# Eleven more tiles turned through DRAM in a linear-attention and NVFP4-GEGLU kernel

## The chip, the core and the metric

The kernel runs on one core of one Trainium2 chip. The metric is device time in microseconds of one execution. Before the change it is 1303.85 us, the median of 3 runs (1300.8 to 1305.99).

## What is computed

Input x has 4 sequences of 512 tokens of width 512. Two pre-norm residual steps are made in float32:

```python
x = x + gated_linear_attention(layernorm(x))     # 4 heads of 128, chunks of 128 tokens
x = x + geglu_mlp(layernorm(x))                  # 512 -> 4096 -> 512, 4-bit weights with scales per block of 32
```

In the attention q, k and v are products of the normed x with 512 x 512 weights; k is scaled to length 1 per head; two gates per head, alpha and beta, come from two further small products. Within a chunk `attn = (q k^T) * beta * decay` and `y_local = attn v`; from chunk to chunk a 128 x 128 state per head is carried, `state = state * total_decay + v^T kw`, and `y = y_local + (q state) * chunk_decay`. In the MLP the weights are unpacked from 4-bit codes, `inter = gelu(x Wg) * (x Wu)`, `out = inter Wd`; every product there is made of three parts (hi, lo, mi) to keep float32 accuracy.

## The kernel before, in words

**Tiles and stages.** All work stands in an order written out by hand; nothing is rescheduled. A counter p numbers the *places*. Each of the 4 sequences b has 12 places: four `product_v`, four `product_q`, four `product_k`. Behind each product, `behind(p)` puts the small work of an earlier chunk: chunk (b, n) has its lead at place 9 + 3 (4b + n), where `chunk_lead` and `chunk_decay` stand, its scores one place later (`chunk_scores`), its sums two places later (`chunk_sums`, which is followed by `second_norm` of the finished rows and by `first_norm` of a tile of the next sequence). From place 45 on the MLP's matmuls take the place of the products, and from about 280 us on the MLP stands alone: 35 rounds of gate, up and down matmuls, with the weights unpacked on VectorE (DVE) and ScalarE (ACT) beside them.

**Turning a tile.** Matmuls contract over the partitions, so a normed tile of 128 tokens x 512 channels must be turned, and k too. Before, there are two ways:

- *On TensorE.* Four `nc.tensor.transpose` into one PSUM bank (L380 for norms, L593 for k), then a copy out of PSUM. All 16 second-norm tiles (`tp_f`) go this way, the 4 first-norm tiles of sequence 0 (`tp_a`), and k of the chunks for which `far(b, n)` is false.
- *Through DRAM.* `cross` writes the tile to DRAM in blocks (one DMA, L310); at the *landing* place it reads it back in four pieces of 64 KB that put 32-row blocks in their turned places (L315); at the *turning* place DVE turns the 32 x 32 blocks (`turn_blocks`, L326). The first-norm tiles of sequences 1 to 3 go this way (`way_a`), and k of chunks 2 and 3 of sequences 0 to 2 (`way_k`).

`cross` books the read at the start of `behind(landing)` (`first_of`) and the turn at its end (`last_of`):

```python
def land():
    t = one_k.get(f"way_{key}")
    for a in range(KC):
        nc.sync.dma_start(f32(t)[:, a * P : (a + 1) * P], way[:, a * 32 : (a + 1) * 32, :])
    last_of.setdefault(turning, []).append(lambda: use(t))
```

A norm that goes through DRAM lands two places after its own and turns three places later. k of a far chunk is written at its product, lands four places ahead of its lead and is turned one place ahead of it.

**Second norm.** `second_norm` (L397 ff.) takes the turned tile, makes its three parts (hi on ACT, L406; lo and mi on DVE, L407 and L408) and stores each to DRAM (`h<-g`, L410). The MLP reads them from there (`x<-h`, L283), the first ones at 202.75 us.

**Queues.** All DMAs are issued by SyncE (SP), in order, on one queue. When a DMA has to wait (the read-back for its write, a store for its data), all later DMAs wait. They run on the core's 16 DMA engines. On SP between 20 and 200 us also stand: x of the next sequences, the residual rows (`xr`) and their write-back (`acc<-xr`), the row sums for the decay (`sums`, read by the exponentials at L608 of the next chunk), the packed MLP weights and their scales, and the h stores. DVE, ACT and TensorE (PE) are in order as well.

**When first norms stand.** `early` (L739 ff.) gives the place of each first norm; for sequence 1 its chunks 0 to 3 stand at places 2, 5, 8 and 8.

Of the kernel before, what the change touches and what calls it, by code (L numbers as in the profile page):

```python
# [35 lines left out]
def f32(t):  # L36
    return t.bitcast(F32)
# [3 lines left out]
def tile_gated_linear_attention__then__nvfp4_geglu(  # L41
# [20 lines left out]
    B, T, D = x.shape  # L62
    H = D // P
    NCH = T // P
# [56 lines left out]
    one_k = Homes("b", 42, [P, T], two_k)  # L121

    def psum(name):
        return fps.tile([P, T], F32, tag="p", name=name)

    def heads(t):
        return t.rearrange("p (h d) -> p h d", d=P)
# [176 lines left out]
    def crossed(t):  # L304
        return t.rearrange("p (w k i) -> p k w i", w=KC, i=32)

    def cross(src, key, use, landing, turning):

        way = dram.tile([KC, P, P], F32, tag=f"way_{key}", name=f"way_{key}")
        nc.sync.dma_start(way.rearrange("w p m -> p w m"), f32(src).rearrange("p (w m) -> p w m", m=P))  # L310
# [7 lines that stand above are left out]
        first_of.setdefault(landing, []).append(land)  # L318

    def turn_blocks(t, *to):  # L320

        new = f32(t).rearrange("p (a k i) -> p k a i", a=KC, i=32)
        done = 0
        for part in to:
            n = part.shape[1]
            nc.vector.transpose(part.rearrange("p k (a j) -> p k a j", j=32), new[:, done : done + n])  # L326
            done += n
        one_k.put(t)

    def norm(src, key, use, parts=1, within=None, way=None):  # L330


        st = small.tile([P, 6], F32, tag="st", name=f"st_{key}")
        nc.vector.bn_stats(st, f32(src))
        if within:
            within()
        mv = small.tile([P, 2], F32, tag="mv", name=f"mv_{key}")
        nc.vector.bn_aggr(mv, st)
        rs = small.tile([P, 1], F32, tag="rs", name=f"rs_{key}")
        nc.vector.tensor_scalar(rs, mv[:, 1:2], 1e-5, None, ALU.add)  # L340
        nc.gpsimd.tensor_tensor(rs, rs, minus_half[:, :1], ALU.pow)

        def settle():

            hn = one_k.get(f"hn_{key}")
            w = D // parts
            if way:
                for c in range(2):
                    nc.vector.tensor_scalar(
                        crossed(f32(hn)).rearrange("p (c two) w i -> p c two w i", c=2)[:, c],  # L350
                        f32(src).rearrange("p (c w i two) -> p c two w i", c=2, w=KC, two=2)[:, c],
                        mv[:, 0:1], rs, ALU.subtract, ALU.mult,
                    )
                one_k.put(src)
                cross(hn, key, way, place[0] + 1, place[0] + 4)
                one_k.put(hn)
                return
            for cols in (slice(i * w, (i + 1) * w) for i in range(parts)):
                nc.vector.tensor_scalar(
                    f32(hn)[:, cols].rearrange("p (c two j) -> p c two j", two=2, j=P),  # L360
                    f32(src)[:, cols].rearrange("p (c j two) -> p c two j", two=2, j=P),
                    mv[:, 0:1], rs, ALU.subtract, ALU.mult,
                )
            one_k.put(src)
            turned.append((hn, key, use))

        settled.append(settle)
# [34 lines left out]
    def second_norm(b, n, src):  # L402
        def use(tp):
            g = [one_k.get(f"g{j}_{b}_{n}") for j in range(3)]
            hi, lo, mi = g
            nc.scalar.activation(hi, tp, AF.Copy, scale=HI)  # L406
            nc.vector.tensor_tensor(lo, tp, f32(hi), ALU.subtract)  # L407
            nc.vector.scalar_tensor_tensor(mi, f32(hi), ONE_E, tp, ALU.mult, ALU.subtract)  # L408
            for j in range(3):
                nc.sync.dma_start(  # L410
                    h2d[b][j][:, :, n * P : (n + 1) * P].rearrange("k p t -> p k t"), heads(f32(g[j]))
                )
            one_k.put(*g)

        norm(src, f"f{b}_{n}", use)


    zs, ss = {}, {}
# [38 lines left out]

    def far(b, n):

        return 1 < n and b < B - 1  # L460

    kTs = {}

    def in_blocks(a):
        return a.rearrange("p (h w i) -> p h w i", h=H, i=32)

    def heads_of(t, blocks):
        return crossed(f32(t)) if blocks else in_blocks(f32(t))

    def product_k(b, n):  # L470

        pk = psum(f"pk_{b}_{n}")
        for k in range(KC):
            nc.tensor.matmul(  # L474
                pk, f32(hT[b][k // 2])[:, k % 2, n * P : (n + 1) * P], f32(wk[k // 2])[:, k % 2, :],
                start=(k == 0), stop=(k == KC - 1),
            )
        kt = one_k.get(f"k_{b}_{n}")
        k_sb[b, n] = kt
        nc.vector.tensor_tensor(heads_of(kt, far(b, n)), in_blocks(pk), in_blocks(f32(bk_sb)), ALU.add)  # L480
        if far(b, n):

            def use(t):
                kT = kTs[b, n] = one_k.get(f"kT_{b}_{n}")
                turn_blocks(t, heads(f32(kT)))

            lead = 2 * NCH + 1 + 3 * (NCH * b + n)
            cross(kt, f"k{b}_{n}", use, lead - 4, lead - 1)
        return lambda: k_factors(b, n, kt)

    def k_factors(b, n, kt):
        sq = one_k.get(f"sq_{b}_{n}")
        sn = small.tile([P, H], F32, tag="ss", name=f"ss{b}_{n}")
        for h in range(H):
            hs = slice(h * P, (h + 1) * P)
            nc.scalar.activation(
                f32(sq)[:, hs].rearrange("p (w i) -> p w i", i=32), heads_of(kt, far(b, n))[:, h],
                AF.Square, accum_out=sn[:, h : h + 1],
            )
        one_k.put(sq)  # L500
        nc.gpsimd.tensor_scalar(sn, sn, 1e-24, None, ALU.max)
        nc.gpsimd.tensor_tensor(sn, sn, minus_half, ALU.pow)
        brn = small.tile([P, H], F32, tag="brn", name=f"brn{b}_{n}")
        nc.gpsimd.tensor_tensor(brn, sn, beta[b][:, n * H : (n + 1) * H], ALU.mult)
        kwf = small.tile([P, H], F32, tag="kwf", name=f"kwf{b}_{n}")
        nc.gpsimd.tensor_tensor(kwf, sn, bdte[b][:, n * H : (n + 1) * H], ALU.mult)
        ss[b, n] = brn, kwf
# [76 lines left out]
    state, ch = {}, {}  # L584

    def chunk_lead(b, n):
        if far(b, n):
            ch["kT"] = kTs.pop((b, n))
            return
        kT = one_k.get(f"kT_{b}_{n}")  # L590
        tp = psum(f"tpk_{b}_{n}")
        for h in range(H):
            nc.tensor.transpose(  # L593
                tp[:, h * P : (h + 1) * P], f32(k_sb[b, n])[:, h * P : (h + 1) * P], ident
            )
        nc.scalar.copy(f32(kT), tp)
        ch["kT"] = kT
# [60 lines left out]
    def chunk_scores(b, n):  # L658
        toks = slice(n * P, (n + 1) * P)
        sp = psum(f"sp_{b}_{n}")  # L660
        kT = ch.pop("kT")
        for h in range(H):
            nc.tensor.matmul(  # L663
                sp[:, h * P : (h + 1) * P], f32(kT)[:, h * P : (h + 1) * P],
                f32(q_sb[b][h // 2])[:, h % 2, toks], start=True, stop=True,
            )
        one_k.put(kT)
        one_k.put(k_sb.pop((b, n)))
        if n == NCH - 1:
            two_k.put(*q_sb[b])  # L670
        if b == B - 1:
            add = state_sums(b, n)
        dm = ch["dm"]
        nc.vector.tensor_tensor(f32(dm), sp, f32(dm), ALU.mult)
        if b == B - 1:
            add()
# [62 lines left out]
    early = {}  # L739
    for b in range(1, B):  # L740
        for n in range(NCH):
            p = 3 * NCH * (b - 1) + 3 * n - 1 if b > 1 else 2 + 3 * min(n, 2)
            early.setdefault(p, []).append((b, n))
    xs = {}

# [6 lines left out]
    def between_steps(p):  # L752

        if p in met:
            return
        met.add(p)
        chunk = chunk_of(p)
        if p % 3 == 0:
            settle()
            if chunk:  # L760
                chunk_lead(*chunk)
                chunk_decay(*chunk)
        elif p % 3 == 1:
            if chunk:
                chunk_scores(*chunk)
            turn("f")
# [8 lines left out]
    def behind(p):  # L775
# [8 lines left out]
        if p % 3 == 0:  # L784
            if left:
                chunk_lead(*chunk)
# [212 lines left out]
    with tc.manual_schedule():  # L999
# [45 lines left out]
        p = 0  # L1045
# [95 lines left out]
```

## Time and profile before

| what | value |
|---|---|
| median of 3 runs | 1303.85 us |
| the profiled execution | 1303.89 us |
| its span, first to last instruction | 1302.2 us |
| mean granted TensorE clock | 0.999 |
| PE busy | 1289.4 us, 99% |
| DVE, ACT, GpSimd (POOL) busy | 968.9, 452.0, 113.6 us |
| `tp_f` matmuls (L380) | 64, four for each of 16 tiles |
| `tpk` matmuls (L593) | 40, four for each of 10 chunks |
| `way_a`, `way_k` writes (L310) | 12 and 6, 256 KB each |
| `way_a`, `way_k` read-backs (L315) | 48 and 24, 64 KB each |
| DVE turns of k (L326, 128 x 512) | 6, median 701 ns |

Matmuls are pipelined, so a row's duration of a matmul is longer than the time from its start to the next one's start; what a matmul takes from the path is read from starts. A view of stretches gives, for each stretch, its length, the busy time of PE, weight loads, DVE, ACT and POOL with the count of instructions, the granted clock, the mean busy share of the 16 DMA engines, and GB/s. A view of waits gives who waited for whom, the sum in us, how often, and the longest.

### The profile page before, as it was taken

Reading aid. Unit: us, or ns where it says so; the run is one execution under the profiler, and the core shown is the slowest. Engines: PE = TensorE matmul, PEld = TensorE weight load, DVE = VectorE, ACT = ScalarE, POOL = GpSimd, SP = SyncE. Lnnn points to the kernel's source line nnn. Section 1 sums busy time; section 2 is a strip of 40 time slices with the busy share of each in tenths; the row PEclk is TensorE's granted clock in tenths of the full one; section 3 lists DMA queues with packets and bytes.
Section 4 is the critical chain, followed back from the end, with each engine's and each line's share of the span. In section 5 each row is a group of like instructions: output and inputs, shape, how many; then the busy total and the mean of one; then the engine's idle time right before and its main releaser. Section 6 shows DMA issues by size and latency. Waiting matters only on the chain.

```text
span 1302.2 us, 17046 instructions
## 1 busy us (share of the span) xinstructions
PE 1289.4 (99%) x5736; PEld 1032.0 (79%) x5736; DVE 968.9 (74%) x1581; ACT 452.0 (35%) x878; POOL 113.6 (9%) x179
## 2 busy tenths in 40 slices
PE   9999999999999999999999999999999999999998
PEld 6567676778888888888888888888888888887886
DVE  3577865888777777777777777777777777777566
ACT  2333335743333333333333333333333333332332
POOL 1536362400000000000000000000000000000000
PEclk9999999999999999999999999999999999999999
DMA  5457677987565656555656565555555555555473
GB/s 195 147 178 195 191 197 214 301 268 235 178 194 178 194 178 194 178 194 179 194 179 193 179 193 179 192 180 192 180 191 181 189 183 189 183 178 198 167 252 127
DMA packets 195383, 250.24 MB, mean 192 GB/s; under 512 B 16672, under 2 KB 93792, under 8 KB 195296
## 3 DMA queue, kind: packets, MB, share of 16 engines
q1 hardware_dynamic: 195296, 249.16, 59.2%
q8 instruction: 45, 0.74, 0.2%
q14 instruction: 42, 0.34, 0.1%
HBM read 191.91 MB, written 57.18 MB: 191 GB/s over the span
## 4 chain that ended last, share of the span: by engine, by line
PE 93%; DMA 3%; DVE 2%; SPq 1%; ACT 1%; issue 0%; POOL 0%; DVEq 0%; ACTq 0%; POOLq 0%
PE pa L853 35%; PE p_d L897 26%; PE pb L853 18%; PE pq L450 4%; PE pk L474 2%; PE pva L425 2%; PE pvb L432 2%; PE yp L717 1%; PE sp L663 1%; PE yp L719 1%; DMA x<-in_x 1%; PE dp L688 1%; DMA pk_d<-in_down_p 1%; PE tp_f L380 0%; DMA x<-h 0%
## 5 line engine op out<-in xcount | busy, mean ns | idle before, releaser
L853 PE MATMUL pa<-x,wgu 128*128 128x512 f32 x2048 | 507.2, 390 | 0.0
L853 PEld LDWEIGHTS pa<-x,wgu 128*128 128x128 f32 x2048 | 384.1, 188 | 79.0
L897 PE MATMUL p_d<-wd,i 128*128 128x512 f32 x1542 | 357.2, 389 | 2.3 <-DVE xr L726 0.6
L897 PEld LDWEIGHTS p_d<-wd,i 128*128 128x128 f32 x1542 | 288.3, 188 | 65.6 <-DVE i L877 2.1
L853 PE MATMUL pb<-x,wgu 128*128 128x512 f32 x1024 | 274.7, 390 | 1.8 <-DMA x<-h 1.8
L858 ACT ACTIVATE t<-pb 128x512 f32<-128x512 f32 x256 | 151.3, 591 | 358.0 <-PE pb L853 353.4
L859 DVE TENSOR_TENSOR t<-pa,t 128x512 f32<-128x512 f32 x256 | 176.6, 690 | 81.2 <-ACT t L858 75.9
L853 PEld LDWEIGHTS pb<-x,wgu 128*128 128x128 f32 x1024 | 192.4, 188 | 42.4 <-DMA x<-h 2.5
L905 DVE SCALAR_TENSOR_TENSOR acc<-p_d,acc 128x512 f32<-128x512 f32 (+1 forms) x137 | 93.4, 682 | 124.8 <-PE p_d L897 123.7
L873 ACT ACTIVATE i<-t 128x512 fp32r<-128x512 f32 x128 | 81.0, 633 | 194.2 <-DVE t L870 189.7
L865 ACT ACTIVATE t<-t 128x512 f32<-128x512 f32 x128 | 81.2, 634 | 136.6 <-DVE t L859 136.5
L877 DVE TENSOR_TENSOR i<-t,i 128x512 fp32r<-128x512 f32 x128 | 88.4, 691 | 25.9 <-ACT i L873 24.1
L909 DVE TENSOR_TENSOR acc<-acc,p_d 128x512 f32<-128x512 f32 x135 | 93.0, 689 | 14.8 <-PE pb L853 0.5
L870 DVE SCALAR_TENSOR_TENSOR t<-t,t 128x512 f32<-128x512 f32 x128 | 88.6, 692 | 4.3
L928 POOL TENSOR_TENSOR acc<-acc,last 128x512 f32<-128x512 f32 x1 | 1.3, 1295 | 1015.0 <-ACT last L927 1015.0
L878 DVE SCALAR_TENSOR_TENSOR i<-i,t 128x512 fp32r<-128x512 f32 x128 | 89.0, 695 | 0.0
L450 PE MATMUL pq<-hT,wq 128*128 128x512 f32 x128 | 57.6, 595 | 0.0
L474 PE MATMUL pk<-wk,hT 128*128 128x512 f32 x128 | 57.4, 593 | 0.0
L450 PEld LDWEIGHTS pq<-hT,wq 128*128 128x128 f32 x128 | 23.6, 191 | 24.1 <-issue 23.9
L474 PEld LDWEIGHTS pk<-wk,hT 128*128 128x128 f32 x128 | 23.3, 191 | 23.9 <-issue 23.9
L183 DVE TENSOR_TENSOR wgu<-wgu,wgu 128x1024 fp32r<-128x1024 f32 x32 | 38.9, 1216 | 0.0
L180 DVE SCALAR_TENSOR_TENSOR wgu<-wgu,w_gu 128x1024 fp32r<-128x1024 f32 x32 | 38.9, 1215 | 0.0
(120 smaller groups left out, 906.0 us busy)
## 6 DMA issues: line engine op xcount, KB each, us to landing
x<-h SPq DMA_DIRECT2D x420, 256.0 KB
acc<-acc SPq DMA_DIRECT2D x256, 256.0 KB
h<-g SPq DMA_DIRECT2D x48, 256.0 KB
x<-in_x SPq DMA_DIRECT2D x16, 256.0 KB
pk_gu<-in_gate_p SPq DMA_DIRECT2D x32, 128.0 KB
sc_gu<-in_gate_s SPq DMA_DIRECT2D x64, 64.0 KB
pk_gu<-in_up_p SPq DMA_DIRECT2D x32, 128.0 KB
sc_gu<-in_up_s SPq DMA_DIRECT2D x64, 64.0 KB
```

The costliest lines, as they stand in the source:

```text
L450: nc.tensor.matmul(pq, f32(wq[k // 2])[:, k % 2, h * P : (h + 1) * P], f32(hT[b][k // 2])[:, k % 2, :], start=(k == 0), stop=(k == KC - 1),)
L474: nc.tensor.matmul(pk, f32(hT[b][k // 2])[:, k % 2, n * P : (n + 1) * P], f32(wk[k // 2])[:, k % 2, :], start=(k == 0), stop=(k == KC - 1),)
L853: nc.tensor.matmul(o, w3[j][:, k % 2, c * P : (c + 1) * P], x[j * KC + k], start=(j == js[0] and k == 0), stop=(j == js[-1] and k == KC - 1),)
L858: nc.scalar.activation(f32(t), pb, AF.Copy, scale=-1.0 / ONE_E)
L859: nc.vector.tensor_tensor(f32(t), pa, f32(t), ALU.add)
L865: nc.scalar.activation(f32(g), f32(g), AF.Gelu_apprx_tanh, scale=ONE_E)
L870: nc.vector.scalar_tensor_tensor(f32(u), f32(g), ONE_E, f32(u), ALU.mult, ALU.mult)
L877: nc.vector.tensor_tensor(il, f32(u), f32(ih), ALU.subtract)
L878: nc.vector.scalar_tensor_tensor(im, f32(ih), ONE_E, f32(u), ALU.mult, ALU.subtract)
L897: nc.tensor.matmul(banks[key_][:, part], inter[i][j][:, n * P : (n + 1) * P], wd[ms[i] // 2][j][:, ms[i] % 2, part], start=(i == 0 and j i ...
L905: nc.vector.scalar_tensor_tensor(a, banks[n, False, part.start][:, part], ONE_E, a, ALU.mult, ALU.add)
L909: nc.vector.tensor_tensor(a, a, banks[n, True, 0], ALU.subtract)
```

## The change

Three things are changed, and no arithmetic but the way in which tiles are turned.

1. The eight second-norm tiles of sequences 0 and 1 go through DRAM. The turned tile is made in SBUF (`h2T`), and its three parts are made from there instead of from PSUM. They are made and stored three places later than before.
2. `far` holds for chunk 1 too, so k of the second chunks of sequences 0 to 2 goes through DRAM. For these the read-back is booked two places ahead of the lead and the turn at the lead, one place ahead of the scores. As the turn now comes after `chunk_lead`, `chunk_scores` takes the turned tile itself.
3. The first norms of sequence 1 stand at places 2, 2, 5 and 8, so those of chunks 1 and 2 stand three places earlier.

On PE, ACT, DVE and SP nothing else changes its order; on POOL nothing changes.

```diff
@@ second_norm
-        norm(src, f"f{b}_{n}", use)
+        def way(t):
+            whole = one_k.get(f"h2T_{b}_{n}")
+            turn_blocks(t, heads(f32(whole)))
+            use(f32(whole))
+            one_k.put(whole)
+
+        norm(src, f"f{b}_{n}", use, way=way if b < 2 else None)
@@ far
-        return 1 < n and b < B - 1
+        return 0 < n and b < B - 1
@@ product_k
-            cross(kt, f"k{b}_{n}", use, lead - 4, lead - 1)
+
+            cross(kt, f"k{b}_{n}", use, *((lead - 4, lead - 1) if n > 1 else (lead - 2, lead)))
@@ chunk_lead
         if far(b, n):
-            ch["kT"] = kTs.pop((b, n))
             return
@@ chunk_scores
-        kT = ch.pop("kT")
+        kT = kTs.pop((b, n)) if far(b, n) else ch.pop("kT")
@@ early
-            p = 3 * NCH * (b - 1) + 3 * n - 1 if b > 1 else 2 + 3 * min(n, 2)
+            p = 3 * NCH * (b - 1) + 3 * n - 1 if b > 1 else 2 + 3 * max(n - 1, 0)
```

## The prediction, made before the changed kernel had run

> **What bounds the kernel now.** I read the page first: engine shares, the 40 slices, the chain that ended last.
>
> ```profile
> PE 1289.4 (99%) x5736; PEld 1032.0 (79%) x5736; DVE 968.9 (74%) x1581; ACT 452.0 (35%) x878; POOL 113.6 (9%) x179
> ...
> DMA  5457677987565656555656565555555555555473
> ...
> PE 93%; DMA 3%; DVE 2%; SPq 1%; ACT 1%; issue 0%; POOL 0%; DVEq 0%; ACTq 0%; POOLq 0%
> ```
>
> TensorE carries the end; every microsecond it stops is a microsecond of the kernel. But the DMA digits are 5 to 9 in slices 1 to 10 (to 325 us), where the change works: an average over 16 engines, behind which a few engines can be full. So next I asked for stretches, and for the DMA queue's waits:
>
> ```profile
> 57.00:60.50 3.50, 3.50 (x20) 3.04 (x19) 2.89 (x9) 1.68 (x6) 3.42 (x6) 1.00 0.29 83
> 233.00:240.00 7.00, 7.00 (x37) 4.90 (x36) 5.41 (x13) 5.77 (x19) 3.80 (x6) 1.00 1.03 363
> 99.00:127.00 28.00, 28.00 (x138) 20.66 (x137) 21.93 (x48) 11.07 (x46) 19.68 (x31) 1.00 0.80 218
> ```
> ```profile
> SPq L315 <- DMA way_a<-hn_a: 26.0, 9, 3.9
> ...
> SPq L310 <- DMA xr<-in_x: 1.1, 1, 1.1
> ```
>
> The last two columns of a stretch are the DMA share and GB/s. From 57 to 60.5 us only read-backs from DRAM run (64 KB pieces, L315): share 0.29 of 16 is 4.6 engines, and 83 GB/s makes a piece 65.5 kB / 83 = 0.79 us; in the trace's semaphore updates they land at 57.39, 58.22, 59.05: 0.82 us apart, one after the other, though issued 0.57 us apart. From 233 to 240 us whole 256 KB loads run on all engines: 262 kB / 363 = 0.72 us each. The last row: from 99 to 127 us the queue is 80% full on average; SP's 1.1 us wait is a write that was held not by its data (hn_a was ready 3 us before) but by an older DMA still in flight.
>
> **A trip through DRAM.** A tile's trip costs the DMA queue one write (0.75 us) and four pieces (4 x 0.82 = 3.3 us): 4.0 us on the few engines that pieces use, and all pieces use the same ones, else they would overlap. SP waits for the write before it issues the pieces (26.0 us in 9 waits: mean 2.9, worst 3.9), and the first data come 2.3 us after that issue (73.09 less 70.07 less 0.8). Everything SP has queued lands behind them.
>
> The Trainium skill (DMA: Bandwidth & Descriptors, Rules for kernel authors, "Use all 16 engines") has a rule against this change: the slowest dimension of an access pattern sets how many engines a DMA gets, and the source here has 4 blocks outermost, so 4 engines. The 4.6 of the row agrees. An estimate from that page's other case, 16 engines: a piece of 0.2 us, eleven trips in 17 us instead of 44, which would fit.
>
> **What goes.** Eight second-norm tiles and three k tiles lose four transposes each, 44 matmuls.
>
> ```profile
> 118.17 0.60 PE L593 MATMUL tpk<-ident,k 128*128 128x128 f32 x4
> 118.61 1.95 PE L425 MATMUL pva<-wva,hT 128*128 128x264 f32 x8
> 120.39 1.89 PE L432 MATMUL pvb<-wvb,hT 128*128 128x256 f32 x8
> 122.12 0.60 PE L380 MATMUL tp_f<-ident,hn_f 128*128 128x128 f32 x4
> 122.55 1.06 PE L663 MATMUL sp<-q,kT 128*128 128x128 f32 x8
> ```
>
> From the start of four to the next matmul: 118.61 - 118.17 = 0.44, 122.55 - 122.12 = 0.43. Eleven times 0.436 is **-4.8 us**, all on the path. ACT's three kT copies (0.58 each) end waits of ACT only: nothing.
>
> **What moves.** The first norm of sequence 1, chunk 2 (and chunk 1) goes three places earlier, into 20 to 45 us, where the queue is nearly empty (share 0.22) and DVE idles 1.7 and 6.9 us at a time; the weights of 36.3 us wait one write longer and are read at 66. That ends one stall:
>
> ```profile
> PE pva L425 <- DVE hT L326: 2.1, 1, 2.1
> ```
>
> Start to start it lost 2.3 us at 63.3 us: **-2.3 us**. But the eight pieces at 53.92 us were those of chunks 2 and 3; now they are chunk 3's and k of chunk 1's.
>
> **What is added on engines.** DVE: eight tiles turn (0.70, the kT row of L326) and normalize in two halves (2 x 0.47 against 0.58), 8 x 1.06, and three kT turns, 2.1: 10.6 us, where DVE is 68% busy (130.0 of the 191 us from 20 to 211). It hides beside the matmuls unless DVE blocks; lo and mi read SBUF in place of PSUM at the same price (691 against 690 ns at L877 and L407). SP: 55 issues of 0.4 to 0.57 us, and eight sets of three stores three places later, which nobody needs before 202 us.
>
> **What is added on the DMA queue.** 11 x 4.0 = 44 us between 49 and 200 us. For the room there, take one stretch without a gap, 98.5 to 114.6 us: pieces 3.3, three h stores 2.3, sums, x, xr, acc, sums 0.7 each, weights 3.2, two writes 1.5 = 13.8 of 16.1 us. The queue has some 15% left, about 20 us of 150; 44 do not fit. So I wrote the new order out by hand at these prices, and compared three deadlines on PE:
>
> - *k chunk 1 of sequence 0.* Written at 48.9 us as chunk 3's tile is now, pieces 5 to 8 of 53.92 us, landed 63.4, turned 64.2. The scores are due at 62.56 - 0.87 = 61.7: a wait of **+2.6 us**, which takes the place of the 2.3 us. Behind DVE's wait for the turn stand the evictions of v's next chunk and dm of the same scores, behind SP's wait sums, x and stores.
> - *k chunk 1 of sequence 1.* Pieces of the pairs f and a (second and first norm): 8 x 0.82 = 6.7 us. Pairs flow at 72.3 to 78.9 and 87.3 to 94.0. Then x, xr, three h, acc and f's write (5.1 us) to 99.1, 2.3 us until data, pair to 108.0. Then sums, x, xr, three h, weights, acc, f's write (9.0) to 117.0; a's and both k writes and sums (2.9) to 119.9; twelve pieces, f, a and k, to 129.9; turn 0.8: 130.7. The scores are due at 122.55 less the 2.7 us won so far = 119.8: **+10.9 us**.
> - *Sequence 2.* From 129.9: x, xr, three h, k's write and pieces, acc, f's write to 139.0, pair to 148.0; the next (k pieces and weights between) to 167.7; the next to 181.6; sums_0 at 182.3, against 167.1 now. From sums to the first yp takes 5 us now (167.19 to 172.09), so 187.3 where PE, 8.2 late less 0.9 won, asks at 179.5: **+7.8 us**. From 182.3: xr, three h, acc, f's write, a, weights, k, sums, k to 191.4, twelve pieces to 201.3, scores at 202.1 instead of 180.98: another **+6.5 us**.
>
> After that no pair is left; the queue has room (share 0.57 from 176 to 200 us), and the rest of the order is as before. **Sum:** the scores start 202.1 - 181.0 = 21.1 us late, in parts -4.8 -2.3 +2.6 +10.9 +7.8 +6.5 = 20.7 (0.4 by rounding). The profiled execution took 1303.9 us (span 1302.2), equal to the median of 1303.85: 1303.9 + 21.1 = **1325.0 us**.
>
> **Costs without a row.** How late a queue that is over full really gets. From below: no lateness but the shortest chain of each k tile. For sequence 1: f written at 107.9, landed 112, twelve pieces 114.2 to 124.1, against 119.8: +4.9; sequence 2 the same way 0 to 3, take 2: -7.1 + 2.6 + 4.9 + 2 = +2.4, 1306.3. From above: pieces at 0.86 (+2), 5 us of DVE blocked behind late pieces that PE must repay, and the clock:
>
> ```profile
> 266.00:269.20 3.20, 1.50 (x6) 0.68 (x4) 2.39 (x4) 2.43 (x6) 1.20 (x2) 1.00 0.91 305
> 269.30:272.70 3.40, 3.40 (x14) 3.30 (x15) 2.38 (x4) 0.64 (x2) 0.71 (x2) 0.50 1.03 342
> ```
>
> Gaps of 1.6 and 0.7 us are followed by 3.4 us at clock 0.50, 1.7 us lost; the 2.3 us gap at 63 us cost no clock. Four new stalls could cost 0 to 6.8 us; those ahead of another stall are absorbed by it. 21.1 + 2 + 5 + 6.8 = +35, 1339. I take the schedule, since its 85% stretch is the nearest row. The Trainium skill (TensorE: Matmul & The Clock Gate, "What's actually happening") says half rate comes after an idle window of some 3.4 us; by that, three of the stalls here would halve it, +5 us.
>
> **Rivals.**
> 1. *Only the tight k trips wait* (the queue catches up in its waits for writes, which now have work beside them). For it: SP waits 26.0 us for writes. Against: these waits are latency, shorter than the added pieces. 1306 to 1315.
> 2. *Not slower:* the pieces overlap with the full loads because twelve engines are idle beside them, and k lands before its scores. Then -4.8 - 2.3, up to 1296.8; with k 2 or 3 us late in each sequence, about 1303. It decides if the twelve pieces ahead of sequence 1's scores land by 119 us. Against: 0.82 us spacing, and in-order landing behind them.
> 3. *DVE blocks in a cascade:* in-order DVE waits for f pieces with TensorE's evictions queued behind; above 1338.
>
> **Chances.** The schedule 0.60 (1315 to 1338); rival 1 0.20; rival 2 0.13 (0.03 of it a gain over 0.5%); rival 3 0.07. A measurement here tells about 0.5%, 6.5 us, from no change: faster 0.03; same (1297.4 to 1310.4) 0.10 + 0.08 of rival 1 = 0.18; slower 0.79. Range 1306 to 1338: it leaves out rival 3 and the part of rival 2 below 1306, under 0.2.
>
> **What would show it.** In the new profile: tp_f x32 and tpk x28; no wait of pva at 63 us; waits of sp L663's line on DVE kT near 62, 120 and 195 us, the second over 8 us; DVE idle before L326, none today; pieces still 0.8 us apart; ACT's dm waiting for sums of sequence 2; from 280 us on the same steps, 21 us later. If pieces of three tiles land in under 5 us, the step on the four engines is wrong; if no kT is late, the deadlines are.

## The result and the profile after

The changed kernel takes 1335.04 us (median of 4 runs, 1333.51 to 1336.59) against 1304.11 us for the kernel before in the same comparison: a ratio of 1.0233, 95% interval 1.0215 to 1.0252. It is slower by 31 us. The forecast was 1325.0, +21; the range of 1306 to 1338 holds the time, near its upper end.

The page of the changed kernel first, the same lines as before (shares of the engines, the granted clock and the DMA share in 40 slices of 33 us, the chain that ended last):

```profile
PE 1293.6 (97%) x5692; PEld 1031.3 (77%) x5692; DVE 976.8 (73%) x1600; ACT 451.2 (34%) x875; POOL 111.3 (8%) x179
...
PE   9996987999999999999999999999999999999998
...
PEclk9999898999999999999999999999999999999999
...
DMA  6565666798646565655565656565656564655463
...
PE 87%; DMA 5%; DVE 3%; SPq 2%; POOL 1%; issue 1%; ACT 1%; DVEq 0%; POOLq 0%; ACTq 0%
```

TensorE runs 44 instructions fewer, as intended. But slices 4 to 7 (100 to 233 us) have holes in PE and in its clock, where before PE worked through; 11% of the chain now belong to DMA, DVE, SP and GpSimd instead of 6%. Everything that happens, happens before 220 us: from there to the end the later start of each step stays between +31 and +33 us. Note the DMA line: in slices 4 to 7 it says 5 and 6, less than before (6 and 7). An average over 16 engines doesn't show that the four which the read-backs use are full (the number is taken up with the wide form below).

The waits of the changed kernel (who waited for whom, sum in us, times, longest). In these views `pva`, `pvb`, `pq` and `pk` are the products v, q and k, `tpk` turns k on TensorE, `sp` are the scores, `yp` the sums; `dm` is the decay, which ACT makes from the row sums (`sums`) and DVE multiplies with the scores:

```profile
ACT dm L614 <- DMA sums<-rows: 42.4, 8, 15.1
...
PE sp L669 <- DVE kT L326: 24.2, 3, 12.6
...
DVE kT L326 <- DMA way_k<-way_k: 19.3, 3, 8.7
...
PE tpk L599 <- DVE k L486: 3.8, 1, 3.8
...
DVE h2T L326 <- DMA way_f<-way_f: 0.6, 1, 0.6
```

The three waits of 24.2 us are the three k tiles of second chunks: 3.1, 12.7 and 8.9 us by starts, at 61.2, 121.7 and 201.2 us. Behind them stands DVE, and behind DVE the read-back of k. The `tpk` row is a fourth wait, which was not foreseen; it is followed up below. The last row says that DVE hardly waited for the pieces of second-norm tiles: 0.6 us in all.

The largest one on PE, and what DVE did meanwhile (changed kernel, in order of time; in brackets the idle time before):

```profile
120.22 1.89 PE L438 MATMUL pvb<-wvb,hT 128*128 128x256 f32 x8
134.66 2.04 PE L669 MATMUL sp<-q,kT 128*128 128x128 f32 x8 [12.55 <-DVE kT L326]
136.50 1.09 PE L431 MATMUL pva<-wva,hT 128*128 128x264 f32 x2
```
```profile
124.95 0.15 DVE L448 TENSOR_TENSOR zs<-pvb,bab_sb 128x8 f32<-128x8 f32 x1
133.81 0.71 DVE L326 STREAM_TRANSPOSE kT<-way_k 128x512 f32<-128x512 f32 x1 [8.71 <-DMA way_k<-way_k]
134.44 0.39 DVE L446 TENSOR_TENSOR v<-pva,bv 128x264 f32<-128x264 f32 x1
```

DVE had nothing to do but wait for the last of twelve read-backs (f, a and k, four each). In the trace's semaphore updates they land between 124.3 and 133.7 us, most of them 0.82 to 0.86 us apart (the last two 1.16 and 0.73). After the wait the scores take 2.04 us in place of 1.06: half the clock.

The stretches (length, busy time of PE, weight loads, DVE, ACT, POOL, the granted clock, the DMA share, GB/s) of the changed kernel at and behind the waits:

```profile
121.00:134.00 13.00, 1.11 (x6) 0.63 (x4) 4.10 (x12) 1.86 (x6) 6.57 (x10) 0.72 0.57 165
134.00:142.00 8.00, 7.34 (x25) 6.30 (x26) 5.50 (x13) 1.58 (x2) 0.06 (x1) 0.60 0.78 231
210.00:220.00 10.00, 9.80 (x49) 8.84 (x50) 6.65 (x16) 2.43 (x6) 0.00 (x0) 0.73 0.84 258
```

While TensorE waits 13 us, the DMA share is 0.57: the queue is the bound and yet 43% of the engines' time is free. And the clock is 0.60 and 0.73 in the stretches in which TensorE works again.

### The profile page after: what moved, and what is told of

Its sections match the earlier page's. It is cut to its first block, busy times and chain, and to the rows that moved or that the text cites. A ratio compares the mean times of both kernels' runs of the same rounds, so it can differ in the third digit from the quotient of the medians.

```text
span 1333.7 us, 17056 instructions
## 1 busy us (share of the span) xinstructions
PE 1293.6 (97%) x5692; PEld 1031.3 (77%) x5692; DVE 976.8 (73%) x1600; ACT 451.2 (34%) x875; POOL 111.3 (8%) x179
## 4 chain that ended last, share of the span: by engine, by line
PE 87%; DMA 5%; DVE 3%; SPq 2%; POOL 1%; issue 1%; ACT 1%; DVEq 0%; POOLq 0%; ACTq 0%
PE pa L859 34%; PE p_d L903 25%; PE pb L859 17%; PE pq L456 3%; PE pk L480 3%; PE pva L431 1%; SPq L315 1%; PE pvb L438 1%; DMA way_k<-way_k 1%; DMA h<-g 1%; PE sp L669 1%; DMA way_f<-hn_f 1%; DMA x<-h 1%; PE yp L723 1%; PE yp L725 0%
## 5 line engine op out<-in xcount | busy, mean ns | idle before, releaser
L883 DVE TENSOR_TENSOR i<-t,i 128x512 fp32r<-128x512 f32 x128 | 88.3, 690 | 26.1 <-ACT i L879 24.2
L669 PE MATMUL sp<-q,kT 128*128 128x128 f32 x128 | 19.1, 297 | 24.2 <-DVE kT L326 24.2
L669 PEld LDWEIGHTS sp<-q,kT 128*128 128x128 f32 x128 | 18.1, 209 | 29.2 <-issue 28.8
```

Source lines behind the costliest of these rows:

```text
L883: nc.vector.tensor_tensor(il, f32(u), f32(ih), ALU.subtract)
```

## What the experiments tell apart

*Theory 1* is the prediction's: the read-backs use a few engines only and are serial there, eleven trips are too many for these, and the k tiles come late because they are the last in line; the half clock after each wait is a term of its own. *Rival A*: only the latency of a k trip (write, then read) is too long for its two places. *Rival B*: DVE, which waits in order for the pieces of f tiles, holds everything behind it. *Rival C* came up with the wide form below: that longer rows in the write do it.

All of them (each one's edit stands in its section below), with the ratio to the kernel before (1304.11 us beside the change, 1302.56, 1302.03 and 1303.00 us in the three groups of four) and, from the starts of PE's matmuls between 10 and 216 us, the sum of the waits over 0.3 us and what the matmuls lost at half clock:

| run | us | ratio (95% interval) | waits, us | half clock, us |
|---|---|---|---|---|
| the change | 1335.04 | 1.0233 (1.0215 to 1.0252) | 30.5 | 8.4 |
| f_only | 1317.02 | 1.0112 (1.0096 to 1.0127) | 16.7 | 4.4 |
| k_only | 1307.66 | 1.0040 (1.0029 to 1.0051) | 5.4 | 1.2 |
| wide | 1297.24 | 0.9960 (0.9945 to 0.9975) | 2.8 | 0 |
| wide_before | 1300.97 | 0.9991 (0.9978 to 1.0003) | 2.3 | 0 |
| busy_wait | 1329.88 | 1.0213 (1.0198 to 1.0228) | 10.3 | 3.1 |
| k_first | 1330.32 | 1.0220 (1.0204 to 1.0235) | 26.0 | 8.7 |
| wide_tight | 1298.14 | 0.9971 (0.9961 to 0.9982) | 2.8 | 0 |
| wide_more | 1307.19 | 1.0042 (1.0029 to 1.0054) | 3.2 | 0 |
| narrow_read | 1331.96 | 1.0226 (1.0210 to 1.0241) | 27.9 | 7.8 |
| wide_f | 1296.42 | 0.9947 (0.9931 to 0.9962) | 0 | 0 |
| homes | 1335.07 | 1.0243 (1.0226 to 1.0260) | 31.5 | 7.7 |
| early_only | 1299.38 | 0.9975 (0.9966 to 0.9984) | 0 | 0 |

### f_only and k_only: the two kinds of tile by themselves

```diff
@@ f_only
-        return 0 < n and b < B - 1
+        return 1 < n and b < B - 1
@@ k_only
-        norm(src, f"f{b}_{n}", use, way=way if b < 2 else None)
+        norm(src, f"f{b}_{n}", use, way=None)
```

> The eight second-norm tiles go through DRAM and the first norms stand early, but k of the second chunks is turned on TensorE as before. Theory 1 (the few engines that read-backs use are over full, and everything that lands late follows from it): eight trips of 4.0 us are 32 us in some 20 us of room, so most of the loss stays, minus the three k trips' 12 us: 1310 to 1322 us, with PE waiting for k of third chunks or for dm (sums) in sequences 1 and 2. Rival A (only the tight k trips wait, since their read-back stands two places ahead): no late kT is left, 1297 to 1302 us. Rival B (DVE's in-order waits for f pieces): close to the changed kernel, 1328 to 1335.

> Only k of the second chunks of sequences 0 to 2 goes through DRAM, and the first norms stand early; all second-norm tiles stay on TensorE. Theory 1 (full engines): three trips of 4.0 us are 12 us in some 20 us of room, so only the chain of each trip can be late: 12 transposes -1.3 us, the 63 us stall -2.3, sequence 0's kT +2.6, others 0 to 3: 1301 to 1306 us. Rival A (tight trips): most of the loss is here, 1315 us or more, with sequence 1's kT over 8 us late. Rival B (DVE behind f pieces): 1301 to 1306 too.

f_only costs 14.5 us, k_only 5.1 (1.7 above the end of what was expected), both together 31. So the whole is more than its parts, as it is with a resource that both draw on. Where the 1.7 us of k_only come from stays open. Rival A falls: with k alone, the scores of sequence 1 wait 0.45 us, with the same two places for the trip. By its price rival B, 25 us or more for f tiles alone, falls too. In k_only (waits of PE):

```profile
PE yp L723 <- DVE dm L680: 2.9, 1, 2.9
...
PE sp L669 <- DVE kT L326: 2.0, 2, 1.7
```

The scores of sequence 0 wait 1.9 us by starts, the term predicted at 2.6; the other row is dm in sequence 2, of which sums come late. In f_only, where no k of a second chunk is in line, another consumer waits (PE's wait, then DVE's ahead of it):

```profile
PE pva L431 <- DVE hT L326: 7.3, 1, 7.3
```
```profile
131.59 0.71 DVE L326 STREAM_TRANSPOSE h2T<-way_f 128x512 f32<-128x512 f32 x1 [7.37 <-DMA h<-g]
```

That is a first-norm tile, which before came in time. Its data were there at 127.9 us, and those of the second-norm tile ahead of it on DVE at 124.5. But DVE could not turn the latter before 131.59: it wanted one of the 42 places in SBUF for a 256 KB tile (a *home*), from which an older h tile was still being stored, and that store, issued at 125.84 us, landed at 131.41. So most of this wait is DVE standing in order, as rival B has it, but for a late store and not for pieces of f tiles. Who waits depends on who stands last; that somebody waits does not.

### wide, wide_before, narrow_read: the same trips on all engines

The tile is written as it stands, in rows of 2 KB, and each of the four read-backs fills 32 partitions instead of a quarter of the columns. Bytes, number of DMAs and places stay the same; besides the rows of the write and the partitions that a read-back fills, its slowest dimension grows from 4 (blocks) to 32 (rows).

```diff
@@ cross
-        way = dram.tile([KC, P, P], F32, tag=f"way_{key}", name=f"way_{key}")
-        nc.sync.dma_start(way.rearrange("w p m -> p w m"), f32(src).rearrange("p (w m) -> p w m", m=P))
+        way = dram.tile([P, KC, P], F32, tag=f"way_{key}", name=f"way_{key}")
+        nc.sync.dma_start(way.rearrange("p w m -> p (w m)"), f32(src))
...
-                nc.sync.dma_start(f32(t)[:, a * P : (a + 1) * P], way[:, a * 32 : (a + 1) * 32, :])
+                nc.sync.dma_start(
+                    f32(t)[a * 32 : (a + 1) * 32, :].rearrange("r (b m) -> r b m", m=P),
+                    way[:, a, :].rearrange("(b r) m -> r b m", r=32),
+                )
```

narrow_read takes this write and leaves the read-back as it was, with the blocks slowest:

```diff
@@ cross
+                nc.sync.dma_start(
+                    f32(t)[:, a * P : (a + 1) * P],
+                    way[a * 32 : (a + 1) * 32, :, :].rearrange("r w m -> w r m"),
+                )
```

> The changed kernel whole, every trip kept in place, but each tile is written to DRAM as it stands (rows of 2 KB) and each of the four read-backs fills 32 partitions, so that its slowest dimension is 32 rows and not 4 blocks; bytes, DMAs and order are the same. Theory 1 (each read-back ran on some four engines, 0.82 us of them): read-backs 0.2 to 0.45 us apart, eleven trips cost about 20 us and fit; the scores wait 0 to 3 us in sequence 0 and hardly later: 1296 to 1304 us, with no stretch at half clock after 100 us. Rival A (latency of the k trips): each keeps its 2.3 us and its write, 1315 us or more. Rival B (DVE): 1325 us or more, since DVE's work is the same.

> The kernel before with the same wide read-backs. Theory 1: nothing in it waited long for its read-backs but one pva (2.1 us), so 1301 to 1305 us; if wide read-backs by themselves gain more, part of what the wide form of the changed kernel gains is not owed to the room. Rivals A and B: the same, 1301 to 1305.

> The changed kernel with the write of the wide form (the tile as it stands, rows of 2 KB) but with read-backs that still fill all 128 partitions from 4 blocks, the blocks slowest. Theory 1 (it is the read-backs' 4 slowest steps that put them on some four engines): 0.8 us apart as before, 1330 to 1338 us. Rival C (the wide form gained by its write of longer rows): 1297 to 1305 us.

This settles it. With wide read-backs the very same change takes 1297.24 us, 38 us less than with narrow ones, and less than the kernel before. The kernel before gains nothing that can be told from them, so it is the added trips that needed the room. With narrow read-backs and the longer rows of the write it takes 1331.96: rival C falls. The stretch of narrow_read that holds hardly anything but read-backs, then the stretches of wide that were shown of the changed kernel:

```profile
101.00:105.00 4.00, 4.00 (x14) 2.00 (x13) 3.71 (x11) 1.68 (x9) 1.39 (x3) 1.00 0.25 76
```
```profile
121.00:134.00 13.00, 13.00 (x67) 9.88 (x66) 12.56 (x29) 3.23 (x10) 6.88 (x8) 1.00 0.81 249
134.00:142.00 8.00, 8.00 (x38) 4.96 (x36) 6.84 (x20) 3.50 (x6) 0.54 (x1) 1.00 0.70 210
210.00:220.00 10.00, 10.00 (x57) 7.53 (x56) 3.74 (x8) 5.85 (x26) 4.21 (x8) 1.00 0.69 219
```

A share of 0.25 is 4 of 16 engines, 76 GB/s for all of them. The semaphore updates say the same of each single read-back: in the changed kernel and in narrow_read all 116 have one update soon after their issue and four as their data land, in wide all 116 have sixteen. In wide the read-backs of two tiles land 0.2 us apart where they had gathered behind a load, and otherwise 0.45 to 0.5 us apart, which is as fast as SP issues them; the stretch from 121 to 134 us has 249 GB/s where the changed kernel had 165, TensorE is busy through all of them, and the clock is 1.00. DVE does the same work as in the changed kernel, 978.8 against 976.8 us, so this work is not the bound. The rule of the Trainium skill that the prediction weighed (DMA: Bandwidth & Descriptors, "Rules for kernel authors", the slowest dimension sets the number of engines) is borne out by these rows.

Of the 4.8 + 2.3 = 7.1 us that should be won (44 transposes and the stall at 63 us), wide wins 5.3 against the kernel before. Two waits of 1.4 us are left, behind DVE's order:

```profile
116.30 0.43 DVE L449 TENSOR_TENSOR v<-pva,bv 128x264 f32<-128x264 f32 x1
116.64 0.41 DVE L450 TENSOR_TENSOR v<-pvb,bv 128x248 f32<-128x248 f32 x1
116.96 0.15 DVE L451 TENSOR_TENSOR zs<-pvb,bab_sb 128x8 f32<-128x8 f32 x1
117.03 0.70 DVE L329 STREAM_TRANSPOSE kT<-way_k 128x512 f32<-128x512 f32 x1
```

k's data had landed at 115.8 us, but its turn stands behind the evictions of a v that TensorE has just finished; the scores start at 117.88, when the turn is done.

### k_first: the same queue, another order in it

```diff
@@ cross
-        first_of.setdefault(landing, []).append(land)
+        at = first_of.setdefault(landing, [])
+        at.insert(0, land) if key[0] == "k" else at.append(land)
```

> The changed kernel, with the read-backs of a k tile issued ahead of those of the norms where both land at one place; nothing else differs. Theory 1 (in sequences 1 and 2, twelve read-backs of 0.83 us on the same engines, k's last): k has its data 8 x 0.83 = 6.6 us sooner, so the waits of 12.7 and 8.9 us shrink to 6 and some 2 to 4; the norms' data come 3.3 us later, which DVE mostly has room for: 1320 to 1330 us. Rival A (the latency of the k trip alone, write and 2.3 us): no change, 1333 to 1337. Rival B (DVE held by f pieces): the same or slower.

The wait of sequence 1 fell from 12.7 to 4.7 us and that of sequence 2 from 8.9 to 2.8, as theory 1 has it, and that of sequence 0 (3.1) is gone. The gain of 14 us and more is not there: all waits together are 26.0 us instead of 30.5, the ratio is 1.022 against 1.0233, and the intervals overlap. The median is 0.3 us above the end of what was expected. In k_first:

```profile
PE sp L670 <- DVE kT L327: 9.4, 4, 4.6
PE yp L724 <- DVE dm L681: 9.3, 3, 3.2
...
PE tpk L600 <- DVE k L487: 4.5, 2, 2.3
```

Three waits for dm and two for k have taken the place; they were 1.8 and 4.0 us in the changed kernel. The two for k stand behind DVE, which waited 5.0 and 3.6 us for homes from which h tiles were being stored. I had counted on room for the norms' pieces. There was none: an order within a full resource only chooses who waits.

### busy_wait: the clock by itself

```diff
@@ chunk_scores
+        for _ in range({(0, 1): 3, (1, 1): 14, (2, 1): 9}.get((b, n), 0)):
+            nc.tensor.matmul(
+                sp, f32(q_sb[b][0])[:, 0, :P], f32(q_sb[b][0])[:, 0, :], start=True, stop=True
+            )
```

> The changed kernel with 3, 14 and 9 needless matmuls of 512 columns (0.858 us each by their spacing in pk) ahead of the scores of the second chunks of sequences 0, 1 and 2, written to the bank that the scores overwrite: 2.6, 12.0 and 7.7 us of work inside waits of 3.1, 12.7 and 8.9 us, so that TensorE doesn't idle there. Theory 1 with the clock as a term of its own: the stretches at half clock after 65, 134 and 210 us go (1.7, 3 and 2.8 us of slowed matmuls in the changed kernel's trace); what was lost ahead of a wait that a DMA ends is absorbed by it, so the whole gains 2.5 to 7 us: 1328 to 1332.5 us. If the clock is no term, 1334 to 1338 us; if the filling collides with the ends of the waits, above 1338.

TensorE now works through the waits, and the clock stays up (busy_wait, the same stretches):

```profile
121.00:134.00 13.00, 12.10 (x30) 5.20 (x29) 3.73 (x10) 1.80 (x5) 6.11 (x10) 1.00 0.57 164
134.00:142.00 8.00, 8.00 (x53) 7.40 (x53) 5.91 (x16) 1.58 (x2) 0.89 (x1) 1.00 0.72 210
```

The queue's rate is what it was (164 against 165 GB/s), and 26 needless matmuls (52 instructions in the trace) bring the end forward, by 5.1 us between the two spans; between the two ratios it is 2.6, and their intervals overlap, so by the times alone the gain is not clear of noise. Against the changed kernel the steps stand 2.1 us earlier after the first wait, 0.9 at the end of the second, 3.7 behind it, 0.2 at 196 us, 1.5 at the end of the third wait, 4.1 behind it, 3.0 at 297 us. (Another 2.1 us come at 302 us, where a wait for h of 1.9 us of the changed kernel is missing here.) What is won at full clock is mostly lost again at the next wait, which a DMA ends; what is won behind the last one stays. So in the trace the clock is a term of its own, worth some 3 us of the end here.

### homes: does the unforeseen wait cost anything?

The fourth wait, tpk's at 175.7 us, comes from here (changed kernel, DVE):

```profile
172.86 0.69 DVE L407 TENSOR_TENSOR g<-h2T,g 128x512 fp32r<-128x512 f32 x1 [0.76 <-ACT g L406]
176.96 0.69 DVE L408 SCALAR_TENSOR_TENSOR g<-g,h2T 128x512 fp32r<-128x512 f32 x1 [3.42 <-DMA h<-g]
...
179.36 0.68 DVE L486 TENSOR_TENSOR k<-pk,bk 128x512 f32<-128x512 f32 x1
```

The tile mi of a second norm wanted a home from which an older h tile was still being stored, as in f_only; the store had been issued at 171.75 us and landed at 176.94. DVE stood, and the eviction of k behind it.

```diff
@@ Homes
-    one_k = Homes("b", 42, [P, T], two_k)
+    one_k = Homes("b", 44, [P, T], two_k)
```

> The changed kernel with 44 homes for 256 KB tiles in place of 42, so that a home is taken again later. It tests the 4.0 us of tpk at 175.7 us, where DVE's mi (L408) waited 3.4 us for the home of an older h tile whose store was late in the queue. If that home is a term of its own, 1330 to 1333 us; theory 1 (what is won there is absorbed by the next wait, which the queue ends at its own time): within 1.5 us of the changed kernel, 1333 to 1337 us.

With two homes more, L408 waits no longer and tpk waits 0.9 us instead of 4.0. The time is 1335.07 us. In homes, from 160 to 200 us:

```profile
PE yp L723 <- DVE dm L680: 6.0, 1, 6.0
```

yp, which waited 1.8 us in the changed kernel, now waits 6.1 for sums that land within 0.5 us of when they did (189.5 us, 189.9 in the changed kernel). The wait was a true one and cost nothing that can be told, because the next one ended at the queue's time. Whether more homes would help f_only, where the home's wait is the largest, no run shows.

### early_only, wide_f, wide_tight, wide_more: what is worth keeping

```diff
@@ early_only, against the kernel before
-            p = 3 * NCH * (b - 1) + 3 * n - 1 if b > 1 else 2 + 3 * min(n, 2)
+            p = 3 * NCH * (b - 1) + 3 * n - 1 if b > 1 else 2 + 3 * max(n - 1, 0)
@@ wide_f, against wide
-        return 0 < n and b < B - 1
+        return 1 < n and b < B - 1
@@ wide_tight, against wide
-            cross(kt, f"k{b}_{n}", use, *((lead - 4, lead - 1) if n > 1 else (lead - 2, lead)))
+            cross(kt, f"k{b}_{n}", use, *((lead - 4, lead - 1) if n > 1 else (lead - 2, lead - 1)))
@@ wide_more, against wide_tight
-        norm(src, f"f{b}_{n}", use, way=way if b < 2 else None)
+        norm(src, f"f{b}_{n}", use, way=way if b < 3 else None)
```

> The kernel before with the early first norms of sequence 1 alone; no tile more goes through DRAM. By the prediction's term the wait of pva on hT at 63.3 us goes and nothing takes its place: -2.3 us, 1300 to 1302 us. If the eight read-backs at one place were no cause of it, 1302 to 1305 us with the wait still there.

> The wide form without k of the second chunks (turned on TensorE as before): the eight second-norm tiles and the early first norms alone. Theory 1: 32 transposes -3.5 us and the stall at 63 us -2.3; the two waits of 1.4 us of the wide form's scores belong to k of the second chunks and go, against 1.3 us of transposes that come back: 1295 to 1299 us, and far below the 1317 us of the same edit with narrow read-backs. If DVE's waits for f pieces are a cost of their own (rival B), 1303 or above.

> The wide form of the changed kernel, with the turn of k of the second chunks booked one place earlier, so that it stands ahead of the evictions of the next v instead of behind them. In the wide form the scores lost 1.4 us twice (116.3 and 173.7 us), behind those evictions. Theory 1 (data are there in time, the wait is DVE's order): both go, 1294 to 1296 us. Otherwise, if the data are the late thing, DVE blocks and it stays at 1297 or above.

> The same, and the four second-norm tiles of sequence 2 through DRAM as well: 16 transposes less, -1.7 us, and four trips more (about 2 us each of the queue). Theory 1: the room is there, 1292.5 to 1295.5 us; where the stretch before 200 us has no room left, or the tiles come too late for the first MLP matmuls, 1297 or above.

early_only: the stall at 63 us is gone, the time is 1299.38 us, 3.3 us less by the ratio; the 2.3 that the trace showed lie within its interval (2.1 to 4.4 us). The median is 0.6 us below what was expected. Of the 5.3 us that wide wins, then, the early first norms alone bring 3.3; what the eleven trips add, 2.1 us between the medians, can't be told from nothing by the ratios.

wide_f: 1296.42 us, the lowest of all, and clear of early_only: 3.0 us for 32 transposes less, which were priced at 3.5. The same edit with narrow read-backs took 1317.02, so 21 us hang on the shape of a read-back. It can't be told from wide (the intervals overlap), and no wait of 1 us or more is left on PE before 260 us: the k tiles of second chunks add nothing that can be measured.

wide_tight missed: 1298.14 us. One of the two waits of the scores went (116 us), the other is 0.8 instead of 1.4, but 0.9 us for a kT at 130.5 and 1.0 us for hT at 181.6 came. For the other, DVE came earlier to a turn whose data were not there yet and waited 3.0 us for them. The kT at 130.5 us was turned when it was in wide (131.0 and 130.8 us), behind the normalizations of two tiles, and TensorE, which had come sooner, waited for it there. What made the wait for hT I did not follow. wide_more missed as well, 1307.19 us: PE is no later than in wide up to 220 us (-0.7), but then, in the first MLP rounds, yp waits 3.4 us for dm at 221.8 us, and ten us are lost by 250 us. Two waits of ACT from 212 to 245 us stand behind it (wide_more):

```profile
ACT i L882 <- DMA h<-g: 5.3, 1, 5.3
ACT dm L617 <- DMA sums<-rows: 4.4, 1, 4.4
```

ACT had to wait for sums before it could make dm, and then for a home from which an h tile was being stored. Both are transfers that came late in the queue; that the four trips more made them late is likely, but no run shows it.

## Why the prediction was right, and where it was too small

- **The bound.** Right. The four engines under the read-backs, not the average share, set the time: wide and narrow_read show it, by the shape of the read-back alone.
- **What goes.** Right. 44 transposes, and the stall at 63 us (early_only).
- **kT of sequence 0, +2.6.** 3.1 us. Its data came at 63.5 us in the trace, 63.4 in the hand-made order.
- **kT of sequence 1, +10.9.** 12.7 us. Its data came at 133.7 against 129.9. The queue was slower than the prices said: the second pair of f and a had landed at 96.2 (94.0 by hand), and what was priced at 9.0 us ahead of the next f's write, weights with their scales among it, took 10.1 (110.5 to 120.7).
- **Sequence 2, +7.8 and +6.5.** The place was right for the second, 8.9 us. The first was shared between tpk (4.0, for a home that was not in the sum) and yp (1.8). sums of sequence 2 landed at 189.9 against 182.3, kT's data at 209.2 against 201.3: from the second pair on, the prices of the queue were some 5% too low (112.9 us in place of 107.3).
- **The queue's prices.** This is the larger of the two terms that were too small. The scores of sequence 2 started at 210.2 us and not at 202.1: 8.1 us of the 10.4 that the forecast lacked between the spans (31.5 against 21.1).
- **The clock.** This is the other one. The prediction took 0 for the clock and left 0 to 6.8 us to the upper bound; the changed kernel's matmuls lose 8.4 us in four stretches (1.7 at 65, 2.6 at 127 to 140, 1.7 at 181, 2.4 at 205 to 215 us). Not all of it reaches the end: the steps stand 29.2 us late at the start of the scores of sequence 2 and 31.9 behind the last stretch, 2.6 more, while the losses ahead of a wait that the queue ends go for the most part into this wait. busy_wait, some 3 us, agrees; as its third wait ended 1.5 us earlier, a part of the 8.1 us may go back to the clock too.
- **Sum.** Along PE's starts, -4.8 - 2.3, waits of 3.1 + 12.7 + 4.0 + 1.8 + 8.9 = 30.5 in place of 27.8, and 8.4 of clock in place of 0 make +31.8, against +31.5 between the two spans. By the dates it is the 21.1 of the forecast, 8.1 more up to the start of those scores, which the queue set, and 2.6 of the clock behind it.
- **Cover by DVE.** Held. Eight tiles and three turns more cost DVE 8 us of busy time (10.6 were priced), and the wide form has the same work with 2.8 us of waits on PE.

Of the rivals of the prediction, the first (only the tight k trips) is refuted by k_only and f_only. Of the third (DVE in a cascade behind f pieces) the changed kernel's trace shows 0.6 us; what DVE did stand for in order, in f_only and in the fourth wait, were homes behind late stores. The second, not slower, named its condition, read-backs that overlap beside idle engines; wide meets it, and the time is then 1297.24 us, where it said up to 1296.8.

## What to carry to other kernels

Before adding transfers to a queue, read the DMA share of a stretch that holds only them: 0.25 with one transfer after the other means four full engines beside an average that looks free, and a reordered access pattern with the rows slowest gives the others back at no cost. If a resource is over full, neither the order in it nor the wait in front of it is worth mending by itself: k_first and homes each removed waits and won nothing clear of noise, since the next consumer waited in their place. A late store keeps its home, so it is a consumer too. Price a new TensorE wait of 3 us or more with its half clock, and where it is the last one in a row, add all of it.

## What the runs showed of the hardware

The half clock goes by slots. In the 14 traces the stretches at half clock that begin between 15 and 320 us (wide and early_only have none; their grid is taken from the stretch at their end) last 3.41 us or two, three or four times that (the changed kernel: 3.41, 13.65, 3.41, 10.24 us). On the grid that their starts give, from 15 to 320 us, 36 slots had TensorE idle for more than 0.55 of their length, and all 36 were followed by a slot at half clock; of 41 slots with 0.3 to 0.55 idle 9 were; of 1175 with less, 3. So a wait of 3.06 us, 2.6 of it inside one slot (61.9 to 65.3 us in the changed kernel, 0.77 idle), halves the clock, and the 2.3 us of the kernel before at 63 us, which fell into two slots, did not; 2.3 us in homes, which ended at 113.4 us and fell mostly into one slot (0.63 idle), did. The Trainium skill (TensorE: Matmul & The Clock Gate, "What's actually happening") describes a free-running window of 3413 ns; that agrees. The prediction reckoned with an idle window; by these slots a window need not be idle as a whole: somewhat over half is enough.
